# Seven products for the output gates of single-node LSTMs, with ScalarE's order held and GpSimd multiplying

## The chip, the cores and the metric

The kernel runs on one core of a Trainium2 chip. The core has TensorE (PE; its weight loads are listed as PEld), VectorE (DVE), ScalarE (ACT), GpSimd (POOL) and SyncE (SP, which issues DMA transfers here). Each takes its own instructions in order; between engines, semaphores make an instruction wait for what it reads or overwrites. The metric is the device time of one execution in microseconds (us), lower is better. Before the change the median of three runs is 2251.39 us (2249.25 to 2252.05).

## The reference

Four graph layers act on x (128 graphs of 64 nodes, 256 features). Each normalizes, applies ReLU, does its work and adds the result to x. The change lies in the third layer (layer 2, counted from 0). After two graph convolutions it runs four passes of LSTMs over windows of p = 1, 2, 3, 4 nodes and replaces the last node of each window by the LSTM's last state:

```python
def step(carry, x_t):
    h, c = carry
    g = x_t @ Wih.T + h @ Whh.T + bias
    i, f, gg, o = jnp.split(g, 4, axis=-1)
    c = jax.nn.sigmoid(f) * c + jax.nn.sigmoid(i) * jnp.tanh(gg)
    h = jax.nn.sigmoid(o) * jnp.tanh(c)
    return ((h, c), None)
...
for p in range(1, MAX_SKIP + 1):
    nw = Tv // p
    wins = h[:, :nw * p, :].reshape(Bv * nw, p, Hd)
    last = _lstm_last(Wih[p - 1], Whh[p - 1], bih[p - 1], bhh[p - 1], wins)
    idx = jnp.arange(nw) * p + (p - 1)
    h = h.at[:, idx, :].set(last.reshape(Bv, nw, Hd))
```

With p = 1 every node is a window, h and c begin at zero, and so there is one step without a forget gate: c = sigmoid(i) * tanh(gg), and the node becomes sigmoid(o) * tanh(c). Everything is float32.

## The kernel before

The kernel is one program without loops at run time. Instructions are written with tiles; a scheduler orders them on each engine by their place in the program and by what is ready in its own model of time, and puts in the semaphores. Three engines are wrapped (Ordered, line 789; Engines, line 811): mark gives the last instruction of TensorE, VectorE and ScalarE, and hold(marks) makes later instructions on an engine be issued behind the one given. GpSimd isn't wrapped. The wrapper's call, line 800, is the line under which nearly all instructions stand in the profile, so groups are told apart by tile names.

The features lie in four tiles big: 128 feature rows, two halves of the features (k), 64 nodes, 32 graphs; nodes(q) gives one. The sixteen blocks of x lie in tiles X0 to X15 of 1024 columns each (begin, line 1503). In layer 2 they are spilled to memory, and while the LSTMs run (windows, line 2268) their space serves as working store: weights, cells c (c_, a Ring, which hands out places in turn), states h, and differences.

A chunk is 16 nodes of one big tile, W = 256 columns for each half (h) of its graphs. In the pass p = 1 there are 16 chunks, taken in pairs; the loop over pairs calls lstm (line 2358) for each. A gate is a product of a 256 x 256 weight with 512 columns: as 2 x 2 blocks eight products of 128 x 128 with 256 columns. gates (line 2385) computes two gates at once with seven products instead. The weights' sums are made in weights (line 2296), the data's differences in the tile T (ls_tx). One set goes so:

- product 1 into bank a; ScalarE copies it to Z (ls_z)
- product 6 into bank b, VectorE adds it to Z; product 7 into bank f, VectorE makes U = Z + f in a part of X15; product 5 into bank d, and U + d is one quarter of the gate tile V (in ls_g)
- product 2 on top of bank a; ScalarE activates it into V: a second quarter
- product 4 on top of bank f, and Z + f is a third quarter; ScalarE activates the two quarters of the upper half k = 1
- product 3 on top of bank d, Z + d is the last quarter, and ScalarE's last activations finish it

Products 4 and 3 add to banks that VectorE has to have read by then; product 2 to one that ScalarE has read. There are seven banks.

Input gate and cell gate of a chunk are one such set. The output gate in p = 1 is computed apart, without savings, by eight of the plain products, as four matmuls of 512 columns (of both halves of the graphs), and activated from its banks. VectorE multiplies c; ScalarE takes tanh; last_state (line 2460) multiplies by the output gate on VectorE and writes the nodes in big, in runs of 16 columns.

The pass p = 2 uses other weight tiles; the weights of p = 3 are loaded into X4 to X7 and X0 to X3 after the first pair of p = 2.

Of the kernel before, what the change touches and what calls it, by code (L numbers as in the profile page):

```python
# [8 lines left out]
F32 = mybir.dt.float32  # L9
I32 = mybir.dt.int32  # L10
AF = mybir.ActivationFunctionType
ALU = mybir.AluOpType
# [901 lines left out]
class Fast:  # L914
# [28 lines left out]
    def act(self, out, a, f, **kw):  # L943
        return self.nc.scalar.activation(out, a, f, **kw)
# [499 lines left out]
B, N, D = 128, 64, 256  # L1444
P = 128
NB = 16
TPB = 4
BT = 512
# [18 lines left out]
class Kernel:  # L1467
# [35 lines left out]
    def begin(self):  # L1503
        nc, o, io = self.nc, self.o, self.io
        self.ident = self.c("ident", P, P)
        make_identity(nc, self.ident)
        self.ones = self.c("ones", P, P)
        nc.vector.memset(self.ones[:], 1.0)
        self.A, self.AT = self.c("A", N, N), self.c("AT", N, N)
        nc.sync.dma_start(self.A[:], io["adj"])  # L1510
        nc.sync.dma_start(self.AT[:], io["adj_t"])
        self.X = []
        for i in range(NB):
            self.X.append(self.c(f"X{i}", P, TPB, D))
        self.load_x(0)

    def load_x(self, i):
# [750 lines left out]
    def windows(self):  # L2268

        nc, o, io = self.nc, self.o, self.io
        cx, (w, wq, gp, tp, zp, psum, pst) = self.stage([("lsw", 1), ("lswq", 1), ("lsg", 2), ("lst", 2), ("lsz", 2),
                                                         ("lsps", 7), ("lstps", 1)], "tile")
        with cx:
            bias = w.tile([P, 4, 8], F32, name="ls_b")
            bh = w.tile([P, 4, 8], F32, name="ls_bh")
            with nc.allow_non_contiguous_dma("a few values"):
                nc.sync.dma_start(bias[:], io["L2_gnn_bih"].rearrange("q (k p) -> p q k", p=P))  # L2280
                nc.sync.dma_start(bh[:], io["L2_gnn_bhh"].rearrange("q (k p) -> p q k", p=P))
            o.add(bias[:], bias[:], bh[:])
            flat = [x[:].rearrange("p t d -> p (t d)") for x in self.X]
# [12 lines left out]
            def weights(p):  # L2296

                out = []
                for n, m in enumerate(("Wih", "Whh") if p > 1 else ("Wih",)):
                    t = load(None, n, None if p % 2 == 0 else 4 - 4 * n)  # L2300
                    ap = io[f"L2_gnn_{m}_t"][p - 1]
                    for kc in range(2):
                        nc.sync.dma_start(t[kc], ap[kc * P:(kc + 1) * P, :])
                    A = [[t[kc].rearrange("p (x k m) -> p x k m", k=2, m=P)[:, :, k, :] for kc in range(2)]
                         for k in range(2)]
                    S1, S2, S4 = (y.rearrange("p (x m) -> p x m", m=P) for y in t[2:5])
                    o.add(S1, A[1][0], A[1][1])
# [4 lines left out]
                    out.append({1: A[0][0], 2: A[0][1], 3: S4, 4: A[1][1], 5: S1, 6: S2, 7: S3,  # L2312
                                "A": A})
                return out

            ready = weights(1)
            for p in range(1, 5):
                Ws = ready
                nw = N // p
                parts = -(-nw // 16)  # L2320
                chunks = []
                for q in range(NG):
                    w0 = 0
                    for k in range(parts):
                        w1 = w0 + (nw - w0) // (parts - k)
# [32 lines left out]
    def lstm(self, p, t, ch, Ws):  # L2358


        o = self.o
        gp, tp, zp, psum, bias = self.lp
        w0, w1, H = ch["w0"], ch["w1"], self.nodes(ch["q"])
        nw = w1 - w0
        W = nw * 16
        at = slice(t + p * w0, t + p * (w1 - 1) + 1, p)
# [17 lines left out]

        def gates(xs, fs):
            G = gp.tile([P, 2, 1024], F32, name="ls_g")
            if p == 1 and len(xs) == 1:
                for k in range(2):
                    ps = psum.tile([P, BT], F32, name="ps")
                    for kc in range(2):  # L2390
                        self.mm(ps[:, 0:2 * W].rearrange("p (w b) -> p w b", b=32), Ws[0]["A"][k][kc][:, xs[0], :],
                                node(kc), kc == 0, kc == 1)
                    self.act(G[:, 0, 2 * W * k:2 * W * (k + 1)].rearrange("p (h w b) -> p h w b", h=2, b=16),
                             ps[:, 0:2 * W].rearrange("p (w h b) -> p h w b", h=2, b=16), fs[0],
                             bias=bias[:, p - 1, 2 * xs[0] + k:2 * xs[0] + k + 1])
# [61 lines left out]
        else:  # L2457
            self.last_state(H, at, W, s(G, 0), s(G, 1))

    def last_state(self, H, at, W, *factors):  # L2460
# [475 lines left out]
```

## Time and profile before

| | |
|---|---|
| median of three runs | 2251.39 us (2249.25 to 2252.05) |
| the profiled execution | 2249.32 us |
| its span | 2247.5 us |
| mean granted TensorE clock | 0.997 of full speed |
| TensorE, VectorE, ScalarE, GpSimd busy, us | 2207.4, 1629.2, 1153.4, 37.9 |
| pass p = 1 on TensorE | about 672 to 825 us |

The span runs from the first to the last instruction; the execution's time also holds what lies around it. Busy time of an engine is the sum of its instructions' time. Matmuls overlap, so the mean duration of one is longer than the distance from one to the next; each float32 matmul of the program is two instructions. Rows of the order of time give start, duration, engine, operation, out<-in, shape and count, and in brackets how long the engine had been idle and what released it. Rows of groups give the count, the busy time and the mean in ns, and the idle time ahead of them.

### The profile page before, as it was taken

Reading aid. Unit: us, or ns where it says so; the run is one execution under the profiler, and the core shown is the slowest. Engines: PE = TensorE matmul, PEld = TensorE weight load, DVE = VectorE, ACT = ScalarE, POOL = GpSimd, SP = SyncE. Lnnn points to the kernel's source line nnn. Section 1 sums busy time; section 2 is a strip of 40 time slices with the busy share of each in tenths; the row PEclk is TensorE's granted clock in tenths of the full one; section 3 lists DMA queues with packets and bytes.
Section 4 is the critical chain, followed back from the end, with each engine's and each line's share of the span. In section 5 each row is a group of like instructions: output and inputs, shape, how many; then the busy total and the mean of one; then the engine's idle time right before and its main releaser. Section 6 shows DMA issues by size and latency. Waiting matters only on the chain.

```text
span 2247.5 us, 33965 instructions
## 1 busy us (share of the span) xinstructions
PE 2207.4 (98%) x12683; PEld 1627.7 (72%) x12683; DVE 1629.2 (72%) x4132; ACT 1153.4 (51%) x2522; POOL 37.9 (2%) x66
## 2 busy tenths in 40 slices
PE   7999998999999999999999999999999999999999
PEld 4554445667987778888999999888888655555654
DVE  8877576888658776676766676656955787777767
ACT  5667865665545663444444444434634664444431
POOL 1000000000220000000000000000000000000000
PEclk9999999999999999999999999999999999999999
DMA  6000210121010000000100002000001000000001
GB/s 181 1 1 17 69 57 23 66 76 30 1 57 1 1 19 1 1 1 1 39 1 1 1 1 70 7 1 1 13 1 55 26 1 15 17 18 20 15 25 48
DMA packets 61071, 54.89 MB, mean 24 GB/s; under 512 B 15203, under 2 KB 58724, under 8 KB 60900
## 3 DMA queue, kind: packets, MB, share of 16 engines
q1 hardware_dynamic: 60900, 52.66, 7.5%
q8 instruction: 101, 1.65, 0.3%
q14 instruction: 70, 0.57, 0.1%
HBM read 35.86 MB, written 16.78 MB: 23 GB/s over the span
## 4 chain that ended last, share of the span: by engine, by line
PE 77%; DVE 5%; ACT 1%; issue 1%; DMA 0%; DVEq 0%; ACTq 0%; SPq 0%
PE ps L800 69%; PE pt L800 4%; PE acc L800 3%; PE pe L800 1%; DVE sm_m L800 1%; DVE X L800 1%; DVE aw L800 1%; DVE XV L800 0%; ACT ls_g L800 0%; ACT h L800 0%; DVE lin_s L800 0%; DVE ls_s L800 0%; DVE lin_p L800 0%; DMA ed_a<-in_L_gnn_a_dram 0%; DVE hT L800 0%
## 5 line engine op out<-in xcount | busy, mean ns | idle before, releaser
L800 ACT ACTIVATE ls_g<-ls_g,ls_b 128x512 f32<-128x512 f32 (+4 forms) x472 | 243.3, 565 | 147.7 <-DVE ls_g L800 145.7
L800 ACT ACTIVATE ls_g<-ps,ls_b 128x256 f32<-128x256 f32 (+3 forms) x268 | 115.4, 470 | 335.4 <-PE ps L800 331.9
L800 PE MATMUL ps<-z,w 128*128 128x512 f32 x512 | 255.5, 621 | 0.0
L800 PE MATMUL ps<-big,X 128*128 128x176 f32 (+3 forms) x848 | 212.9, 367 | 0.1
L800 DVE TENSOR_TENSOR ls_g<-ls_z,ps 128x512 f32<-128x512 f32 (+5 forms) x258 | 147.4, 577 | 90.3 <-PE ps L800 88.6
L800 PE MATMUL ps<-ls_tx,X 128*128 128x160 f32 (+2 forms) x960 | 207.0, 327 | 1.6 <-DVE ls_tx L800 0.9
L800 PE MATMUL ps<-X,X 128*128 128x160 f32 (+2 forms) x918 | 205.8, 308 | 0.0
L800 PE MATMUL ps<-X,ls_w 128*128 128x256 f32 x640 | 190.6, 379 | 0.1
L800 PEld LDWEIGHTS ps<-ls_tx,X 128*128 128x128 f32 x960 | 161.8, 190 | 16.4 <-DVE X L800 4.8
L800 DVE TENSOR_TENSOR aw<-at,ed_OST 128x1024 f32<-128x1024 f32 x128 | 150.3, 1220 | 28.7 <-PE ps L800 28.5
L800 PEld LDWEIGHTS ps<-big,X 128*128 128x128 f32 x848 | 146.1, 190 | 29.6 <-issue 19.1
L800 ACT ACTIVATE r<-ps 128x512 f32<-128x512 f32 x256 | 129.3, 625 | 74.4 <-PE ps L800 74.3
L800 DVE TENSOR_TENSOR X<-ls_g 128x1024 f32<-128x1024 f32 (+2 forms) x108 | 117.5, 1088 | 50.6 <-ACT ls_g L800 50.6
L800 PEld LDWEIGHTS ps<-X,X 128*128 128x128 f32 x918 | 152.8, 190 | 0.6
L800 PE MATMUL ps<-X,ls_s 128*128 128x256 f32 x480 | 142.8, 379 | 0.0
L800 PEld LDWEIGHTS ps<-z,w 128*128 128x128 f32 x512 | 87.0, 190 | 66.6 <-issue 59.5
L800 PE MATMUL ps<-ls_tx,ls_s 128*128 128x256 f32 x464 | 134.9, 380 | 0.0
L800 PEld LDWEIGHTS ps<-X,ls_w 128*128 128x128 f32 x640 | 121.5, 190 | 16.6 <-DVE X L800 0.5
L800 PE MATMUL ps<-ls_tx,ls_w 128*128 128x256 f32 x464 | 133.4, 380 | 0.0
L800 PE MATMUL ps<-big,ls_w 128*128 128x256 f32 x464 | 132.0, 380 | 0.7 <-ACT ls_z L800 0.7
L800 PE MATMUL ps<-ed_S,Q 64*128 64x512 f32 x512 | 121.0, 604 | 0.9 <-DVE X L800 0.9
L800 PE MATMUL ps<-aw,ed_ODT 128*32 128x512 f32 x1024 | 121.7, 593 | 0.1
(575 smaller groups left out, 4010.4 us busy)
## 6 DMA issues: line engine op xcount, KB each, us to landing
X<-in_x_dram SPq DMA_DIRECT2D x32, 512.0 KB
xs<-X SPq DMA_DIRECT2D x16, 512.0 KB
X<-xs SPq DMA_DIRECT2D x16, 512.0 KB
out_dram<-X SPq DMA_DIRECT2D x31, 256.0 KB
X<-in_L_gnn_Wih_t_dram SPq DMA_DIRECT2D x4, 512.0 KB
ls_w<-in_L_gnn_Wih_t_dram SPq DMA_DIRECT2D x4, 512.0 KB
ls_w<-in_L_gnn_Whh_t_dram SPq DMA_DIRECT2D x4, 512.0 KB
w<-in_L_gnn_W_t_dram SPq DMA_DIRECT2D x2, 512.0 KB
```

Source lines behind the costliest of these rows:

```text
L800: i = method(*a, **kw)
```

## The change

It concerns the pass p = 1 alone, which gets a function of its own, single, for a pair of chunks.

- A pair runs three sets of seven products: input and cell gate of the first chunk, those of the second, and the output gates of both chunks (the same weights, two data). The eight plain products go, and with them the weights' entry "A".
- The gate tiles come from a ring of four, each two X tiles (X8 and X9, X10 and X11, X12 and X13, X0 and X1). For that, X is allocated in eight tiles of two blocks, and X[i] is a half of one. T comes from a ring of three: X2, X3, X14.
- Instructions can be put off in the list late. The next set runs them right after its copy Z, and a hold puts ScalarE's part of them behind that copy: the last activations of a set, and the tanh of a cell, which follows one set after its product.
- GpSimd multiplies the cells, and the states in last_state. In the last pair the states are multiplied by VectorE, and the list is emptied at the end.
- In the output set two chunks share a bias, so one activation takes both.

```diff
-        self.X = []
-        for i in range(NB):
-            self.X.append(self.c(f"X{i}", P, TPB, D))
+        self.X2 = [self.c(f"X{i}", P, 2, TPB, D) for i in range(0, NB, 2)]
+        self.X = [x[:, i] for x in self.X2 for i in range(2)]
...
+            self.late = []
+            self.g_ = Ring([self.X2[i][:].rearrange("p x t d -> p x (t d)") for i in (4, 5, 6, 0)])
+            self.t_ = Ring([flat[i] for i in (2, 3, 14)])
...
+                    if p == 1:
+                        self.single(two, Ws[0], n + 2 >= len(chunks))
+                        continue
...
-            if p == 1 and len(xs) == 1:
-                for k in range(2):
-                    ps = psum.tile([P, BT], F32, name="ps")
-                    for kc in range(2):
-                        self.mm(ps[:, 0:2 * W].rearrange("p (w b) -> p w b", b=32), Ws[0]["A"][k][kc][:, xs[0], :],
-                                node(kc), kc == 0, kc == 1)
-                    self.act(G[:, 0, 2 * W * k:2 * W * (k + 1)].rearrange("p (h w b) -> p h w b", h=2, b=16),
-                             ps[:, 0:2 * W].rearrange("p (w h b) -> p h w b", h=2, b=16), fs[0],
-                             bias=bias[:, p - 1, 2 * xs[0] + k:2 * xs[0] + k + 1])
-                return G
...
+    def single(self, two, A, last):
+        nc, o = self.nc, self.o
+        _, _, zp, psum, bias = self.lp
+        I, F, G, O = range(4)
+        data = []
+        for ch in two:
+            H, at = self.nodes(ch["q"]), slice(ch["w0"], ch["w1"])
+            T = self.t_.next().rearrange("p (n w b) -> p n w b", n=4, b=16)
+            o.sub(T[:, 0:2], H[:, :, at, 16:32], H[:, 0, at, :].rearrange("p w (h b) -> p h w b", h=2))
+            o.sub(T[:, 2], H[:, 1, at, 16:32], T[:, 0])
+            o.sub(T[:, 3], H[:, 1, at, 0:16], T[:, 2])
+            data.append({1: H[:, 0, at, 0:16], 2: H[:, 1, at, 0:16], 3: H[:, 1, at, 16:32],
+                         5: T[:, 0], 7: T[:, 1], 6: T[:, 2], 4: T[:, 3]})
+
+        def gates(pairs, act):
...
+            a = product(1, "a", True)
+            self.act(Z, a, AF.Copy)
+            nc.hold((None, None, nc.mark()[2]))
+            while self.late:
+                self.late.pop(0)()
+            nc.hold()
+            o.add(Z, Z, product(6, "b", True))
+            o.add(U, Z, product(7, "f", True))
+            o.add(V[:, :, 1, 1], U, product(5, "d", True))
+            a = product(2, "a", False)
+            act(V[:, :, 0, 0], a, 0)
+            o.add(V[:, :, 1, 0], Z, product(4, "f", False))
+            act(V[:, :, 1], V[:, :, 1], 1)
+            o.add(V[:, :, 0, 1], Z, product(3, "d", False))
+            self.late.append(lambda: act(V[:, :, 0, 1], V[:, :, 0, 1], 0))
+            return tile
+
+        def apart(out, a, k):
+            for i, (x, f) in enumerate(((I, AF.Sigmoid), (G, AF.Tanh))):
+                self.act(out[:, i], a[:, i], f, bias=bias[:, 0, 2 * x + k:2 * x + k + 1])
+
+        def together(out, a, k):
+            self.act(out, a, AF.Sigmoid, bias=bias[:, 0, 2 * O + k:2 * O + k + 1])
+
+        def cell(V):
+            def product():
+                nc.gpsimd.tensor_tensor(V[:, 0], V[:, 0], V[:, 1], op=ALU.mult)
+                soon.append(lambda: self.act(V[:, 1], V[:, 0], AF.Tanh))
+            self.late.append(product)
+
+        cells, soon = [], []
+        for b in data:
+            V = gates(((I, b), (G, b)), apart)
+            self.late += soon
+            soon.clear()
+            cell(V)
+            cells.append(V)
+        V = gates([(O, b) for b in data], together)
+        self.late += soon
+        for i, ch in enumerate(two):
+            self.late.append(lambda i=i, ch=ch: self.last_state(
+                self.nodes(ch["q"]), slice(ch["w0"], ch["w1"]), 256, V[:, i], cells[i][:, 1],
+                engine=None if last else nc.gpsimd))
+        if last:
+            while self.late:
+                self.late.pop(0)()
+
+    def last_state(self, H, at, W, *factors, engine=None):
...
-            self.o.mul(y, *(x[:, 2 * W * k:2 * W * (k + 1)].rearrange("p (h w b) -> p h w b", h=2, b=16) for x in factors))
+            (engine or self.nc.vector).tensor_tensor(y, *(x[:, 2 * W * k:2 * W * (k + 1)].rearrange("p (h w b) -> p h w b", h=2, b=16) for x in factors), op=ALU.mult)
```

More of the change, by code (lines that the diff above doesn't have):

```diff
@@ L2282, in windows @@
             o.add(bias[:], bias[:], bh[:])
-            flat = [x[:].rearrange("p t d -> p (t d)") for x in self.X]
+            flat = [x.rearrange("p t d -> p (t d)") for x in self.X]
+            self.late = []
+            self.g_ = Ring([self.X2[i][:].rearrange("p x t d -> p x (t d)") for i in (4, 5, 6, 0)])
+            self.t_ = Ring([flat[i] for i in (2, 3, 14)])
             self.c_, self.h_, self.th_ = Ring(flat[12:15]), Ring(flat[8:10]), Ring(flat[10:12])
@@ L2311, in weights @@
                     o.sub(S3, A[0][0], A[1][0])
-                    out.append({1: A[0][0], 2: A[0][1], 3: S4, 4: A[1][1], 5: S1, 6: S2, 7: S3,
-                                "A": A})
+                    out.append({1: A[0][0], 2: A[0][1], 3: S4, 4: A[1][1], 5: S1, 6: S2, 7: S3})
                 return out
@@ L2458, in lstm, with product @@
             self.last_state(H, at, W, s(G, 0), s(G, 1))
-    def last_state(self, H, at, W, *factors):
+    def single(self, two, A, last):
[12 more added lines that the diff above has]
+        def gates(pairs, act):
+            tile = self.g_.next()
+            V = tile.rearrange("p x (k h w) -> p x k h w", k=2, h=2)
+            banks = {}
+            def product(m, bank, first):
+                if first:
+                    banks[bank] = psum.tile([P, 2, 256], F32, name="ps")
+                for i, (x, b) in enumerate(pairs):
+                    nc.tensor.matmul(banks[bank][:, i, :].rearrange("p (w b) -> p w b", b=16), A[m][:, x, :], b[m],
+                                     start=first and i == 0, stop=i == 1, skip_group_check=True)
+                return banks[bank][:]
+            Z = zp.tile([P, 2, 256], F32, name="ls_z")[:]
+            U = self.u_.next().rearrange("p (x w) -> p x w", x=2)
+            a = product(1, "a", True)
[40 more added lines that the diff above has]
+                self.late.pop(0)()
```

## The prediction

> **What bounds the kernel now.** I read the page first, for the engine that sets the time.
>
> ```profile
> PE 2207.4 (98%) x12683; PEld 1627.7 (72%) x12683; DVE 1629.2 (72%) x4132; ACT 1153.4 (51%) x2522; POOL 37.9 (2%) x66
> ...
> PE 77%; DVE 5%; ACT 1%; issue 1%; DMA 0%; DVEq 0%; ACTq 0%; SPq 0%
> ```
>
> TensorE is busy 98% of the span and carries 77% of the chain that ended last. But a busy TensorE says little of its rate, so next come stretches of the stage that changes (columns: stretch, length, then busy time and count of PE, PEld, DVE, ACT, POOL, the granted clock, DMA).
>
> ```profile
> 672.19:692.67 20.48, 19.49 (x75) 13.53 (x73) 18.88 (x33) 12.28 (x21) 0.00 (x0) 1.00 0.06 26
> 702.15:711.63 9.48, 9.48 (x38) 6.86 (x37) 7.09 (x11) 5.77 (x11) 0.00 (x0) 1.00 0.00 0
> 860.00:880.00 20.00, 20.00 (x94) 17.64 (x93) 10.71 (x16) 6.34 (x12) 0.00 (x0) 1.00 0.00 1
> ```
>
> The single-node stage starts at 672.2 with a pair of chunks that takes 20.48 us; after it every chunk takes 9.48 us, with TensorE always busy and the clock at 1.00. Each matmul of the program is two instructions here. A chunk issues 28 instructions of 256 columns (14 for input and cell gate, seven products each) and 8 of 512 columns (output gate, no saving). If a 512 costs two 256, that is 44 units in 9.48 us, 0.2155 us a unit; the two-node stage behind (94 instructions of 256 in 20 us) gives 0.2128. So the steady stage is limited by TensorE's issue rate, and a unit removed is worth 0.213 to 0.2155 us, so long as nobody makes TensorE wait.
>
> Who could is seen in the order of time of one chunk.
>
> ```profile
> 703.01 2.75 PE L800 MATMUL ps<-ls_tx,X 128*128 128x256 f32 x12
> 703.21 0.60 ACT L800 ACTIVATE ls_z<-ps 128x512 f32<-128x512 f32 x1 [0.18 <-PE ps L800]
> 704.14 0.69 DVE L800 TENSOR_TENSOR ls_z<-ls_z,ps 128x512 f32<-128x512 f32 x1 [0.55 <-PE ps L800]
> 704.78 1.29 DVE L800 TENSOR_TENSOR big<-ls_g 128x512 f32<-128x512 f32 x2
> 705.99 0.68 DVE L800 TENSOR_TENSOR X<-ls_z,ps 128x512 f32<-128x512 f32 x1
> 706.78 0.69 DVE L800 TENSOR_TENSOR ls_g<-X,ps 128x512 f32<-128x512 f32 x1
> 707.32 1.03 PE L800 MATMUL ps<-ls_tx,X 128*128 128x256 f32 x4
> 708.39 0.69 DVE L800 TENSOR_TENSOR ls_g<-ls_z,ps 128x512 f32<-128x512 f32 x1 [0.92 <-PE ps L800]
> 709.11 1.33 ACT L800 ACTIVATE ls_g<-ls_g,ls_b 128x512 f32<-128x512 f32 x2 [1.55 <-DVE ls_g L800]
> ```
>
> A set of seven products is a conversation: copy Z, three VectorE sums, and only then may products 4 and 3 go into banks that those sums read. The answer comes 0.2 to 0.27 us after the last matmul of a product. Now the output gate's eight instructions lie in these gaps. After the change nothing of that kind is left to fill them.
>
> **The change, part by part.** All per pair of chunks, eight pairs.
>
> *TensorE.* Output gates of two chunks: 16 instructions of 512 (32 units) become 28 of 256. 88 units become 84: 4 × 0.2155 = 0.86 us, or 0.85 by the lower rate. Over eight pairs -6.8 to -6.9 us; I take **-6.9**. The pair falls from 18.96 to 18.1 us, a set of seven to 6.03, a product to 0.86.
>
> *VectorE.* The rows for the prices (line group: shapes, count, busy, mean ns, idle before):
>
> ```profile
> L800 DVE TENSOR_TENSOR X<-ls_g 128x1024 f32<-128x1024 f32 x13 | 15.9, 1226 | 10.2 <-ACT ls_g L800 10.2
> L800 DVE TENSOR_TENSOR big<-ls_g 128x512 f32<-128x512 f32 x26 | 16.8, 689 | 0.1
> L800 ACT ACTIVATE ls_g<-X 128x1024 f32<-128x1024 f32 x13 | 13.6, 1048 | 0.0
> ...
> L2168 POOL TENSOR_TENSOR X<-a 128x512 f32<-128x512 f32 x11 | 13.9, 1267 | 264.6 <-ACT a L800 264.6
> ```
>
> Two cell products (1.226) and four state products (0.689) leave: -5.2. Three sets of five sums replace two sets: five more of 0.686, +3.4. From 14.2 busy (2 × 7.09) to 12.4 of 18.1: 69%. The final pair keeps its four state products on VectorE, 2.8 us, behind which only the next stage's sums queue.
>
> *ScalarE.* Four output activations of 0.676 leave (-2.7); a copy of 0.597, one activation of 512 from PSUM at 0.676, one of 1024 at 1.048 and one of 512 at 0.714 come (+3.0). 11.5 becomes 11.9 of 18.1: 66%. The hold places the previous set's last activations, and a tanh of 1.05, behind the new copy. What waits for them is a GpSimd product, a tanh one set later, or a state that a following set's tile reuse needs 2 us later. Nothing of TensorE's waits there. In front of the copy stay the activations of the upper half, 1.33 us for two, which start when the sum after product 4 ends: 0.06 into the next set. So copy at 1.4 to 2.0, sums at 2.05, 2.8 and 3.65, the last ending at 4.33. Product 4 is due at 4.30 and needs the second sum (3.5), product 3 at 5.16 needs the third: slack 0.8 us each. That cover hides all ScalarE edits; a copy 1 us later costs about 0.2 us a set.
>
> *GpSimd.* Two products of 1024 and four of 512. From 1.267 at 512 and 0.763 at 256 the first come to 2.3 us, an estimate. 2 × 2.3 + 4 × 1.27 = 9.7 of 18.1 us: 54%, in order: four state products, then one product in each of the next two sets. The first product has about 3 us until its tanh is queued, the rotating gate tiles (four) are written again about 2 us after the state product read them. Hidden, if GpSimd is alone.
>
> Against the move stands a rule: the Trainium skill, GPSIMD Engine Reference, § 4.1 Engine selection, gives elementwise products to VectorE, GpSimd being about 2 times slower. The row here says 1.84 (1267 over 689 ns), and left on VectorE they would make 17.6 busy of 18.1 us with a chain of waits in it, some 0.5 us of stall a set; so by the rule most of the gain would go, by the trace the move is needed.
>
> *GpSimd beside VectorE.* The trace shows one way in which they meet (order of time, layer 2):
>
> ```profile
> 557.74 1.27 POOL L2168 TENSOR_TENSOR X<-a 128x512 f32<-128x512 f32 x1 [193.76 <-ACT a L800]
> 559.08 2.32 POOL L2168 TENSOR_TENSOR X<-a,X 128x256 f32<-128x256 f32 x2
> 560.74 0.68 DVE L800 TENSOR_TENSOR n_r<-n_r,n_v 128x4 f32<-128x4 f32 x1
> ...
> 588.88 0.69 DVE L800 TENSOR_TENSOR y<-pt,w_b 128x512 f32<-128x512 f32 x1 [2.15 <-PE pt L800]
> ```
>
> The tiny n_r product, 0.16 us elsewhere, took 0.68 and ended at 561.42, as the GpSimd pair did (561.40): with both inputs in SBUF it sat until GpSimd was through. The y sum, one input from PSUM, took its usual 0.69 under a GpSimd instruction. So the sums of the products are free of this, and the six differences a pair of the T tiles (two of 0.685, four of 0.42, both inputs in SBUF) are not. VectorE is in order: a blocked difference holds the sums behind it, and those hold products 4 and 3. VectorE has two gaps of about 1.1 us a set; a difference leaves some 0.3 us of one, with 0.8 of slack that is 1.1 us of cover. A state product (1.27) is nearly always covered; a cell product can block up to 2.3, 1.2 beyond the cover. Ends: 0, and two such full blocks a pair, 2.4 us, 19 us in all. Cell products hold 26% of the time and some four groups of differences fall anywhere, so one hit a pair; its mean excess is 1.2² / (2 × 2.3) = 0.3. The differences become free only as the output set's products have read their tiles, 1 us or more into a cell product, so I take half, 0.15 a pair: **+1.2**.
>
> *Start.* The first pair of 20.48 loses 1.5 over the steady rate; 0.9 of it is TensorE waiting for ls_tx, whose space came free late. T now lies in X2, X3 and X14, free after the last layer-2 products at about 666. But eight weight sums (0.69, SBUF inputs) run in that pair and can meet GpSimd's first products. Between -1.5 and +1.5, **-0.4** taken, half of the wait.
>
> *X in pairs of tiles* adds no instruction; the halves don't overlap, so loads and spills of one need not wait for the other. SP's transfer of the third pass's second weight set into X0 to X3 now waits for the last states, some 4 us; used a whole pass later, its price is VectorE waiting in its sums, 0 to +1. I take 0.
>
> Sum: -6.9 + 1.2 - 0.4 = **-6.1 us**. The profiled execution took 2249.32 (span 2247.5 and 1.8 around it), which would become 2243.2; the median of the runs is 2.07 above it, so I predict 2251.39 - 6.1 = 2245.3.
>
> **The rivals.** *The lock eats the gain.* Groups of differences land in full cell products: 1.2 a pair, +9.6 instead of +1.2, so +2.3 in all; half as bad is -1.9. About 2251. For it: a cell product is as long as the two VectorE gaps together. Against: 31% idle VectorE.
>
> *Slower: GpSimd becomes a bound.* The state products write H in runs of 16 elements; the row of 1.267 has runs of 256. If that doubles them to 2.5, GpSimd is at 14.8 of 18.1 us and every difference meets it: each of four groups waits 0 to 2.5 us, a mean excess over the cover of 1.4² / (2 × 2.5) = 0.4, 1.6 a pair; with products late for their tanh about 2, so +16, and 2260. It decides from 0.86 + 0.05 + 0.56 = 1.5 us a pair on.
>
> *The hold doesn't bind.* With last activations still ahead of the copy it is 0.95 us later, 0.15 beyond the slack, 0.45 a pair, +3.6: 2249. With the tanh too (two sets in three) 1.2 in each, 2.5 a pair, +20: 2265. Against it: it is a plain order on one engine.
>
> **How the numbers follow.** Forecast 0.62, its own range 2242.8 to 2246.9; lock 0.21; GpSimd bound 0.10; hold 0.07. About 0.2% (4.5 us) is what a measurement can tell from no change. Faster by more: 0.62; slower: 0.10, 0.02 of the lock's and 0.02 of the hold's; within: 0.24. The range runs from -6.9 - 1.5 (2243, no stall and the start's whole loss back) to a little above the lock's 2251; what it leaves out is the GpSimd bound and the worse ends, 0.17.
>
> **What would show it.** Right: about 18.1 us from pair to pair, TensorE issuing 84 instructions in it, GpSimd about 54% busy, state products near 1.27. The lock: T differences far above 0.69 and 0.42 ending with GpSimd instructions, and TensorE waiting for VectorE's X or ls_g. The GpSimd bound: state products of 2 us and more. The hold: copies starting behind a tanh. Wrong altogether, if a time outside this stage moves by more than 2 us.

## The result: 0.23% slower, and the profile after

The changed kernel takes 2255.94 us (median of nine runs, 2252.99 to 2259.09), the kernel before, beside it, 2251.39. The ratio is 1.0023 with a 95% interval of 1.0015 to 1.0032: some 5 us slower, where 6 us faster were forecast. The profiled execution of after took 2253.03 us.

The page of after, its span, its engines and the chain that ended last, in which the time can't be seen yet:

```profile
span 2251.2 us, 34215 instructions
...
PE 2200.3 (98%) x12779; PEld 1641.8 (73%) x12779; DVE 1633.4 (73%) x4128; ACT 1155.1 (51%) x2522; POOL 112.5 (5%) x110
...
PE 74%; DVE 5%; issue 2%; ACT 1%; POOL 0%; DMA 0%; POOLq 0%; DVEq 0%; ACTq 0%; SPq 0%
```

TensorE is busy for 7.1 us less than before, as it should be with fewer columns to multiply, and the span is still 3.7 us longer. TensorE's share of the chain fell from 77% to 74%, which suggests that it now waits for somebody. Stretches of the stage, the first three pairs and one of the later ones (stretch, length, then busy time and count of PE, PEld, DVE, ACT, POOL, the granted clock, DMA):

```profile
669.94:689.97 20.03, 18.39 (x85) 15.87 (x84) 18.06 (x24) 11.06 (x19) 4.80 (x2) 1.00 0.01 1
689.97:712.47 22.50, 19.31 (x86) 15.53 (x84) 17.82 (x28) 11.94 (x21) 9.85 (x6) 1.00 0.00 0
712.47:733.90 21.43, 18.93 (x86) 15.70 (x85) 15.57 (x25) 11.73 (x21) 9.95 (x6) 1.00 0.00 1
792.00:811.37 19.37, 18.40 (x85) 15.88 (x84) 14.13 (x21) 11.80 (x21) 9.97 (x6) 1.00 0.00 1
```

84 instructions a pair are what was forecast (a window counts one more at its edge), but in place of the 18.1 us forecast the pair in the last row takes 19.37 us, and the second and third pair take 22.50 and 21.43. The clock is at 1.00 throughout, so the time goes into waits. Which, the waits of the stage tell (engine, tile and line; what it waited for; us in total, times, the longest):

```profile
POOL X L2513 <- DVE ls_z L800: 33.2, 12, 3.6
...
PEld ps L800 <- DVE X L800: 13.8, 10, 2.0
...
PE ps L800 <- DVE X L800: 9.8, 10, 1.6
DVE ls_tx L800 <- POOL big L2539: 4.0, 2, 2.6
...
PE ps L800 <- ACT ls_z L800: 1.5, 2, 1.1
```

TensorE waits ten times for VectorE's results in X (the gate tiles and U), and VectorE itself twice for nodes that GpSimd writes. The order of time shows both, and how regular they are. First an output set in the steady part (start, duration, engine, operation; in brackets the idle time ahead of it and what ended it):

```profile
805.97 2.36 POOL L2513 TENSOR_TENSOR X<-X 128x1024 f32<-128x1024 f32 x1 [3.63 <-DVE ls_z L800]
806.02 0.69 DVE L800 TENSOR_TENSOR X<-ls_z,ps 128x512 f32<-128x512 f32 x1
...
806.62 2.27 DVE L800 TENSOR_TENSOR X<-big 128x512 f32<-128x512 f32 x1
...
808.81 0.68 DVE L800 TENSOR_TENSOR X<-X,ps 128x512 f32<-128x512 f32 x1
...
809.54 1.99 PE L800 MATMUL ps<-big,X 128*128 128x256 f32 x8 [0.97 <-DVE X L800]
```

The second row is the sum U, the fourth the third sum, which has to read its bank before product 3 (the last row) may add to it. Between the two stands a difference for a T tile, X<-big. It takes 2.27 us instead of 0.69 and ends half a microsecond after GpSimd's cell product. Product 3 waits, and the set takes 7.29 us instead of 6.04: 1.25 us lost. The third sum would otherwise have stood at about 807.22 (806.02 + 1.20, the distance in a run below); it came 1.59 later and TensorE lost 1.25 of that, so the cover at this place was only 0.34 us.

The meeting is no accident. GpSimd's cell product reads what ScalarE's last activations of a set write; in 15 of 16 cases it starts 0.08 or 0.13 us after they end (0.48 at 742.24). The hold puts these activations behind the next set's copy Z, and that set's first sum (ls_z) waits for the copy too. In the steady pairs the two end within 0.02 us of each other, so the profile puts 12 of the 16 waits down to ls_z; that it isn't the releaser shows at 678.12, where the product starts 0.27 us before the first sum ends. So the product starts as the first sum ends, U follows that sum, and the difference follows U. The same happens in six output sets, 1.24 to 1.30 us each.

Second, the start of the stage and the first state products:

```profile
678.12 2.35 POOL L2513 TENSOR_TENSOR X<-X 128x1024 f32<-128x1024 f32 x1 [19.90 <-ACT X L800]
678.31 2.71 DVE L800 TENSOR_TENSOR ls_s<-ls_s,ls_w 128x512 f32<-128x512 f32 x1
...
681.67 1.13 PE L800 MATMUL ps<-X,X 128*128 128x256 f32 x4 [1.64 <-DVE X L800]
...
692.11 5.13 POOL L2539 TENSOR_TENSOR big<-X,X 128x512 f32<-128x512 f32 x4 [2.75 <-ACT X L800]
...
697.27 0.69 DVE L800 TENSOR_TENSOR ls_tx<-big 128x512 f32<-128x512 f32 x1 [1.43 <-POOL big L2539]
...
713.43 5.23 POOL L2539 TENSOR_TENSOR big<-X,X 128x512 f32<-128x512 f32 x4 [4.00 <-ACT X L800]
...
718.70 0.69 DVE L800 TENSOR_TENSOR ls_tx<-big 128x512 f32<-128x512 f32 x1 [2.61 <-POOL big L2539]
...
722.35 1.13 PE L800 MATMUL ps<-big,X 128*128 128x256 f32 x4 [1.08 <-ACT ls_z L800]
```

The first cell product blocks a weight sum (ls_s, 2.71 us for 0.69) and costs TensorE 1.9 us. The other rows are a wait that was not there before: the differences for the first chunks of the *next* pass (ls_tx) stand in VectorE's queue in the middle of p = 1. They read nodes that the state products write. Those products are now on GpSimd and end later, and VectorE, which takes its queue in order, stands idle 1.43 and 2.61 us with this pass's sums behind.

The groups of VectorE in the stage (count, busy time, mean ns, idle ahead), and then those of GpSimd, put sizes to it:

```profile
L800 DVE TENSOR_TENSOR X<-big 128x512 f32<-128x512 f32 x13 | 18.5, 1420 | 0.0
...
L800 DVE TENSOR_TENSOR X<-big,X 128x256 f32<-128x256 f32 x26 | 13.5, 520 | 0.3
```

```profile
L2513 POOL TENSOR_TENSOR X<-X 128x1024 f32<-128x1024 f32 x16 | 37.8, 2365 | 68.7 <-ACT X L800 35.5 <-DVE ls_z L800 33.2
L2539 POOL TENSOR_TENSOR big<-X,X 128x512 f32<-128x512 f32 x28 | 36.3, 1324 | 26.7 <-ACT X L800 26.7
```

**The account.** The length of the stage, from TensorE's first product of p = 1 to its first of p = 2, was 153.15 us and is 159.56: +6.4. A set without a stall takes 6.04 us; what the sets take above that is:

| what TensorE lost to | us |
|---|---|
| a difference of 512 columns behind a cell product, six output sets | 7.6 |
| a difference of 256 columns behind state products, second pair | 1.8 |
| ls_tx behind GpSimd's states, second and third pair | 3.3 |
| the weight sum behind the first cell product | 1.9 |
| sum | 14.6 |

Against it stand 6.9 us of saved matmuls and 1.5 us that the first pair had lost before: -6.9 - 1.5 + 14.6 = +6.2, of 6.4 measured. The last pair, which has no differences left to make, runs at 6.05 and 6.04 us a set.

The stage's length is the better measure in what follows, for the execution's time carries a scatter from ahead of the stage: the same instructions at the start of layer 2 began anywhere between 500.4 and 505.8 us in the twelve profiles (503.5 before, 500.6 after: 2.9 us that hide a part of the 6.4 in the two profiled executions).

### The profile page after: what moved, and what is told of

It reads as the page before. It is cut to its first block, busy times and chain, and to the rows that moved or that the text cites. A ratio compares the mean times of both kernels' runs of the same rounds, so it can differ in the third digit from the quotient of the medians.

```text
span 2251.2 us, 34215 instructions
## 1 busy us (share of the span) xinstructions
PE 2200.3 (98%) x12779; PEld 1641.8 (73%) x12779; DVE 1633.4 (73%) x4128; ACT 1155.1 (51%) x2522; POOL 112.5 (5%) x110
## 4 chain that ended last, share of the span: by engine, by line
PE 74%; DVE 5%; issue 2%; ACT 1%; POOL 0%; DMA 0%; POOLq 0%; DVEq 0%; ACTq 0%; SPq 0%
PE ps L800 67%; PE pt L800 4%; PE acc L800 3%; DVE X L800 2%; PE pe L800 1%; DVE sm_m L800 1%; DVE aw L800 1%; POOL big L2539 0%; ACT X L800 0%; DVE XV L800 0%; ACT ls_g L800 0%; ACT h L800 0%; ACT big L800 0%; DVE ls_z L800 0%; DVE lin_s L800 0%
## 5 line engine op out<-in xcount | busy, mean ns | idle before, releaser
L800 PE MATMUL ps<-X,X 128*128 128x160 f32 (+2 forms) x1302 | 296.7, 329 | 3.8 <-DVE X L800 3.8
L800 ACT ACTIVATE ls_g<-ls_g,ls_b 128x512 f32<-128x512 f32 (+5 forms) x408 | 207.9, 559 | 126.1 <-DVE ls_g L800 123.8
L800 PEld LDWEIGHTS ps<-X,X 128*128 128x128 f32 x1302 | 225.3, 190 | 15.7 <-DVE X L800 5.4
L800 ACT ACTIVATE ls_g<-ps,ls_b 128x256 f32<-128x256 f32 (+2 forms) x204 | 80.5, 438 | 303.7 <-PE ps L800 302.5
L800 PE MATMUL ps<-big,X 128*128 128x256 f32 (+2 forms) x816 | 182.1, 334 | 7.5 <-DVE X L800 5.9
L800 DVE TENSOR_TENSOR ls_g<-ls_z,ps 128x512 f32<-128x512 f32 (+3 forms) x226 | 125.5, 561 | 76.1 <-PE ps L800 74.3
L800 PEld LDWEIGHTS ps<-big,X 128*128 128x128 f32 x816 | 139.1, 190 | 18.8 <-DVE X L800 8.3
L800 PE MATMUL ps<-ls_tx,X 128*128 128x160 f32 (+1 forms) x704 | 146.2, 307 | 0.6 <-ACT ls_g L800 0.6
L800 DVE TENSOR_TENSOR X<-ls_z,ps 128x512 f32<-128x512 f32 (+4 forms) x185 | 112.7, 610 | 41.8 <-PE ps L800 37.9
L800 DVE TENSOR_TENSOR X<-ls_g 128x1024 f32<-128x1024 f32 (+2 forms) x92 | 97.9, 1064 | 38.9 <-ACT ls_g L800 38.9
```

Of the source, the lines that this page charges most:

```text
L800: i = method(*a, **kw)
```

## The experiments

Two mechanisms were suspected: the *lock* (a VectorE instruction with both inputs in SBUF sits until GpSimd is through) and the *queue* (ls_tx ahead of this pass's sums, waiting for GpSimd's states). The rivals were that the three sets of seven products are themselves too tight, that VectorE has too much work, and that ScalarE's hold costs more than it gives. All edits are to the changed kernel. Each ratio is to runs of the kernel before that were made beside the run, whose medians lie between 2248.74 and 2251.39 us, so times of different rows are compared by their ratios.

| kernel | stage, us | time, us | ratio to before (95%) |
|---|---|---|---|
| before | 153.15 | 2251.39 | 1 |
| after | 159.56 | 2255.94 | 1.0023 (1.0015 to 1.0032) |
| differences with an operand from PSUM | 149.56 | 2246.64 | 0.9980 (0.9971 to 0.9990) |
| ls_tx put off | 157.29 | 2254.30 | 1.0017 (1.0007 to 1.0027) |
| all products on VectorE | 144.87 (145.8) | 2240.64 | 0.9957 (0.9940 to 0.9974) |
| no hold | 169.61 | 2266.03 | 1.0066 (1.0049 to 1.0083) |
| cells on VectorE | 157.11 (158.1) | 2255.26 | 1.0025 (1.0015 to 1.0034) |
| states on VectorE | 156.85 | 2254.67 | 1.0023 (1.0012 to 1.0034) |
| differences on GpSimd | 158.10 | 2257.61 | 1.0039 (1.0025 to 1.0053) |
| all on VectorE, no hold | 145.00 (145.9) | 2239.56 | 0.9967 (0.9954 to 0.9980) |
| differences on GpSimd, ls_tx put off | 148.12 | 2245.25 | 0.9985 (0.9976 to 0.9995) |
| the seven products alone | 143.79 (145.6) | 2243.37 | 0.9967 (0.9956 to 0.9979) |

In four runs the schedule puts the first matmuls of p = 2 ahead of the last four of p = 1 (eight in the last run), so there the stage as measured ends early. The end of p = 1 in the last run shows it (matmuls with ls_w belong to p = 2):

```profile
817.62 0.59 PE L800 MATMUL ps<-big,ls_w 128*128 128x256 f32 x2
818.05 1.05 PE L800 MATMUL ps<-X,X 128*128 128x256 f32 x4
818.94 0.59 PE L800 MATMUL ps<-big,ls_w 128*128 128x256 f32 x2
819.38 1.09 PE L800 MATMUL ps<-big,X 128*128 128x256 f32 x4
```

In brackets is the time to the last matmul of p = 1, less that of the matmuls of p = 2 before it. Comparisons go by these.

### The lock: differences with one operand from PSUM

```diff
-            o.sub(T[:, 0:2], H[:, :, at, 16:32], H[:, 0, at, :].rearrange("p w (h b) -> p h w b", h=2))
-            o.sub(T[:, 2], H[:, 1, at, 16:32], T[:, 0])
-            o.sub(T[:, 3], H[:, 1, at, 0:16], T[:, 2])
+            o.sub(T[:, 0:2], H[:, :, at, 16:32], self.flat0[:, 0:512].rearrange("p (k w b) -> p k w b", k=2, b=16))
+            o.sub(T[:, 2], T[:, 0], self.flat0[:, 0:256].rearrange("p (w b) -> p w b", b=16))
+            o.sub(T[:, 3], T[:, 2], self.flat0[:, 256:512].rearrange("p (w b) -> p w b", b=16))
```

(flat0 is a bank of zeros in PSUM; the tiles T then hold no differences, and the output is not the reference's.)

> The six differences a pair take their second operand from a PSUM bank of zeros, so that they have one input in SBUF (the products then get wrong data, and the output is not the reference's); their number, shapes and engine stay. Measured by the stage's length, from TensorE's first product of p = 1 to its first of p = 2 (before 153.1 us, after 159.6). Lock theory (a difference with two SBUF inputs sits until GpSimd's instruction ends, and holds the sums behind it): the differences return to 0.69 and 0.42 us, the stall of 1.25 us in each output set (six of them, 7.6 us) and the one of 1.8 in the second pair go, the stage is 150 +- 1.5, the time 9 us under the changed kernel and 4 under the one before. Rival (VectorE's order alone: a difference stands between the second and the third sum and delays product 3 whatever GpSimd does): differences are already 0.7 us, the stage stays within 2 us of 159.6.

The stage took 149.56 us, 10.0 less than after, where the account gives 7.6 + 1.8 = 9.4 to the lock. The groups of VectorE in this run, and then the same place in the order of time:

```profile
L800 DVE TENSOR_TENSOR X<-X,pt 128x256 f32<-128x256 f32 x31 | 13.0, 418 | 1.1
L800 DVE TENSOR_TENSOR X<-big,pt 128x512 f32<-128x512 f32 x15 | 10.2, 680 | 0.0
```

```profile
710.41 0.69 DVE L800 TENSOR_TENSOR X<-ls_z,ps 128x512 f32<-128x512 f32 x1
710.42 2.38 POOL L2515 TENSOR_TENSOR X<-X 128x1024 f32<-128x1024 f32 x1 [2.92 <-DVE ls_z L800]
...
711.01 0.68 DVE L800 TENSOR_TENSOR X<-big,pt 128x512 f32<-128x512 f32 x1
...
711.61 0.68 DVE L800 TENSOR_TENSOR X<-X,ps 128x512 f32<-128x512 f32 x1
```

The difference stands between the same two sums, with a cell product running on GpSimd, and takes 0.68 us: 1420 became 680 ns, 520 became 418, and the output set takes 6.04. So neither the order on VectorE nor the count of its instructions makes the stall, but the second operand in SBUF. This is what the Trainium skill says (SBUF — State Buffer, § Who interferes with whom): a VectorE instruction with two SBUF inputs contends with a GpSimd instruction that reads SBUF; one with a single SBUF input, outside the 2-port modes, does not.

### The queue: ls_tx put off

```diff
+        if p == 2 and t == 0:
+            self.nc.hold((None, self.guard, None))
         o.sub(T[:, 0:2], H[:, :, at, 16:32], half(0))
...
+        self.nc.hold()
...
+        self.guard = nc.mark()[1]
         V = gates([(O, b) for b in data], together)
```

> Only the differences of the next pass's first two chunks (ls_tx) are issued later on VectorE, behind the sums that precede the last output set of p = 1; in the changed kernel they stand in the second and third pair, where VectorE waits for GpSimd's states that they read. Queue theory (VectorE in order waits there 1.4 and 2.6 us and lets products 2 and 4 come late): the sets that are 1.3 and 2.0 us too long become 6.04, the stage is 156.3 +- 0.7, the time 3 us under the changed kernel. Rival (those two stalls come from the lock on the differences around them): the stage stays at 159.6 within 0.7.

157.29 us: 2.3 gained of the 3.3. Up to the end of p = 1 only the ls_tx rows moved in VectorE's order. Both sets, 7.33 and 8.05 us in after, take 6.04, as the queue theory has it. What is missing is a new stall of 1.2 us in the last set, where one of the moved rows meets a cell product (1.98 us for 0.42). The pair of runs with GpSimd's differences below tests the same edit on a longer wait.

### Nothing on GpSimd

```diff
             def product():
-                nc.gpsimd.tensor_tensor(V[:, 0], V[:, 0], V[:, 1], op=ALU.mult)
+                o.mul(V[:, 0], V[:, 0], V[:, 1])
...
-                engine=None if last else nc.gpsimd))
+                engine=None))
```

> Cells and states are multiplied by VectorE, nothing by GpSimd; all else as changed. Lock theory: no difference is longer than 0.75 us and no wait for GpSimd is left, but VectorE has 17.6 us of work for 18.1; with waits in its chain about 0.3 us are lost a set, 19 us a pair, the stage is 153 +- 3, so 4 to 9 us under the changed kernel, near the one before. Rival (the move to GpSimd is worth more than the lock costs, as the prediction had it): the stage is 162 or more, slower than the changed kernel.

144.87 us (145.8 with the last matmuls), 7 better than expected, and 2240.64: of the runs so far that compute everything, the first that beats both kernels, by 0.4% over the one before. A long stretch of the stage in this run, and then the same stretch of before:

```profile
690.00:800.00 110.00, 110.00 (x510) 95.86 (x509) 103.84 (x171) 70.97 (x120) 0.00 (x0) 1.00 0.00 1
```

```profile
690.00:800.00 110.00, 110.00 (x420) 79.58 (x419) 82.54 (x129) 68.40 (x118) 0.00 (x0) 1.00 0.00 1
```

TensorE never waits in 110 us and issues 510 instructions, of 256 columns each. VectorE's rows cover 94% of the stretch, yet TensorE doesn't wait for it. (The busy time of a stretch counts a moment once, however many rows cover it; it is not the sum of the rows, as was said ahead of the prediction. Their sum here is 115.3 us.) Two groups of this run, and four state products in its order of time:

```profile
L800 DVE TENSOR_TENSOR X<-X 128x1024 f32<-128x1024 f32 x16 | 19.5, 1221 | 0.4 <-ACT X L800 0.3
...
L800 DVE TENSOR_TENSOR X<-big 128x512 f32<-128x512 f32 x13 | 8.9, 687 | 0.1
```

```profile
692.48 2.50 DVE L800 TENSOR_TENSOR big<-X,X 128x512 f32<-128x512 f32 x4
```

The differences are back at 687 ns, and a cell product costs VectorE 1.22 us where GpSimd takes 2.36. Four products of 0.688 each took 2.50 us together: they start 0.60 apart, so the rows overlap, and both their sum and the time that they cover overstate how full VectorE is.

### The hold

```diff
             self.act(Z, a, AF.Copy)
-            nc.hold((None, None, nc.mark()[2]))
             while self.late:
                 self.late.pop(0)()
-            nc.hold()
```

> The hold on ScalarE is left out: last activations, the tanh and the rest of the list may be issued ahead of the next set's copy. If the hold binds and matters, copies start 0.9 us later or more in most sets and the stage grows by 0.45 a pair, 3.6 us, to 163. If the scheduler puts the copy first anyway, or the 0.8 us of slack covers it: within 1 us of 159.6. The lock theory expects the stall of 1.25 in the output sets unchanged in both.

169.61 us, 10.0 more than after, where 3.6 were expected. The order of time, two tanh rows on ScalarE:

```profile
773.94 1.06 ACT L800 ACTIVATE X<-X 128x1024 f32<-128x1024 f32 x1 [2.52 <-POOL X L2511]
...
780.69 1.06 ACT L800 ACTIVATE X<-X 128x1024 f32<-128x1024 f32 x1 [2.47 <-POOL X L2511]
```

Without the hold ScalarE takes a tanh while its product is still on GpSimd, and stands for 2.5 us with the activations of the current set and the next copy behind it. In the four steady pairs whose output sets stall this costs 3.4 us more than in after. The other 6.7 lie in the first three pairs, and not all of them are ScalarE's: VectorE's order changed as well (ls_tx stands ahead of a third sum and waits 5.6 us instead of 4.0; a difference of the first pair now meets a cell product), and twice the granted clock was at half for 3.4 us, which the run with GpSimd's differences explains below. How the 6.7 divide was not tried. With GpSimd multiplying, the hold is needed. Whether it is worth anything by itself, the same edit without GpSimd tells:

```diff
-            nc.hold((None, None, nc.mark()[2]))
...
-            nc.hold()
...
-                nc.gpsimd.tensor_tensor(V[:, 0], V[:, 0], V[:, 1], op=ALU.mult)
+                o.mul(V[:, 0], V[:, 0], V[:, 1])
...
-                engine=None if last else nc.gpsimd))
+                engine=None))
```

> Nothing on GpSimd and no hold on ScalarE. With GpSimd the hold was worth 10 us of stage, since without it a tanh that waited 2.5 us for GpSimd's product stood ahead of ScalarE's other work. If that wait was the cause, the hold is worth little here: stage 145 to 147, as with the hold (144.9). If the copy's place alone is what counts, as the prediction reckoned it: 148 to 155.

145.00 against 144.87 us (145.9 against 145.8): nothing. The hold pays for a delay that the move to GpSimd made.

### One half of GpSimd's work each

Cells on VectorE, states on GpSimd:

```diff
-                nc.gpsimd.tensor_tensor(V[:, 0], V[:, 0], V[:, 1], op=ALU.mult)
+                o.mul(V[:, 0], V[:, 0], V[:, 1])
```

> Cells are multiplied by VectorE, states still by GpSimd. Lock theory: what blocked the difference of 512 in each output set for 2.3 us was the cell product, so those stalls (1.25 each) go; a state product blocks at most 1.27, mostly covered; the next pass's differences still wait for GpSimd's states (2 to 3 us in all). Stage 149 +- 2 (changed kernel 159.6, nothing on GpSimd 144.9), time about 10 us under the changed kernel. Rival (VectorE fuller by 2.4 us a pair is late for the chain): stage 155 or more.

157.11 us (158.1 with the last matmuls), and 149 was expected: a miss. The groups of VectorE, and the order of time of one pair:

```profile
L800 DVE TENSOR_TENSOR X<-big,X 128x256 f32<-128x256 f32 x26 | 21.6, 830 | 0.0
...
L800 DVE TENSOR_TENSOR X<-big 128x512 f32<-128x512 f32 x13 | 9.0, 710 | 0.1
```

```profile
793.75 5.53 POOL L2539 TENSOR_TENSOR big<-X,X 128x512 f32<-128x512 f32 x4 [14.25 <-ACT X L800]
...
794.21 1.10 DVE L800 TENSOR_TENSOR X<-big,X 128x256 f32<-128x256 f32 x1
...
795.83 0.91 DVE L800 TENSOR_TENSOR X<-big,X 128x256 f32<-128x256 f32 x1
```

The 512 differences are free, as they no longer meet cell products. But the 256 ones now stand in VectorE's order behind the first state products and meet all four, one after the other: 0.83 us on average instead of 0.42. By this trace the lock moved to other instructions with the schedule. The wait of ls_tx stayed too, at 4.2 us. The states on VectorE, cells on GpSimd:

```diff
-                engine=None if last else nc.gpsimd))
+                engine=None))
```

> States are multiplied by VectorE, cells still by GpSimd. Lock theory: the cell product goes on blocking the difference in the output set, about 1.25 us a pair, and the weight sum in the first pair, 1.9; the waits of the next pass's differences for GpSimd go. Stage 145 + 7.6 + 1.9 = 154.5 +- 2, time about 5 us under the changed kernel. Rival (the states' four blocks a pair are the greater part): stage 148 or less.

156.85 us, where 154.5 with a margin of 2 was expected: 0.35 beyond it. VectorE's group in this run:

```profile
L800 DVE TENSOR_TENSOR X<-big 128x512 f32<-128x512 f32 x13 | 18.7, 1440 | 0.0
```

The cell products block the 512 differences as in after (1440 ns), some 1.3 us in each output set. There is no wait for ls_tx, since VectorE writes the nodes itself. Neither half alone brings the kernel under the time before.

### GpSimd makes the differences as well

If the lock is between GpSimd and VectorE's differences, giving GpSimd the differences too removes it, at the price of more work on GpSimd and later states.

```diff
-            o.sub(T[:, 0:2], H[:, :, at, 16:32], H[:, 0, at, :].rearrange("p w (h b) -> p h w b", h=2))
...
+            sub = lambda out, a, b: nc.gpsimd.tensor_tensor(out, a, b, op=ALU.subtract)
+            sub(T[:, 0:2], H[:, :, at, 16:32], H[:, 0, at, :].rearrange("p w (h b) -> p h w b", h=2))
...
```

> The six differences a pair go to GpSimd as well, where no lock can meet them; products stay on GpSimd, which then has 15.3 us of work for 18.1 in one queue, while VectorE keeps only sums with a PSUM input (and the eight weight sums). Lock theory: no VectorE instruction in the steady pairs is longer than 0.75 us, and the stall of 1.25 in each output set goes; what is left is GpSimd being late with a difference or a product. Stage 147 to 153. Rival (GpSimd's own queue is what is slow): stage above 158, TensorE or ScalarE waiting for GpSimd.

158.10 us, above what was expected and just the rival's number. But GpSimd's queue is slow in the first pairs alone. In a steady stretch of this run TensorE has no wait:

```profile
730.00:790.00 60.00, 60.00 (x278) 52.77 (x277) 34.38 (x50) 38.86 (x66) 46.28 (x37) 0.99 0.00 1
```

Sets take 6.04 and 6.05 us there, 77% of GpSimd's time being busy. All is lost in the first three pairs: 1.9 us at the weight sum, and two sets of 11.75 and 11.49 us, whose wait on VectorE is

```profile
DVE ls_tx L800 <- POOL big L2540: 10.3, 2, 5.4
```

GpSimd makes differences ahead of its state products, so ls_tx waits 10.3 us for them instead of 4.0. TensorE in turn stands still for 3.7 and 3.2 us, and what follows each time is part of the price (the first of the two; then two stretches of the same length behind it):

```profile
703.14 1.93 PE L800 MATMUL ps<-big,X 128*128 128x256 f32 x4 [3.74 <-ACT ls_z L800]
```

```profile
703.33:706.74 3.41, 3.41 (x9) 2.50 (x9) 1.85 (x3) 1.40 (x4) 2.36 (x1) 0.50 0.00 0
706.74:710.15 3.41, 3.41 (x18) 3.00 (x17) 2.00 (x3) 2.59 (x6) 0.00 (x0) 1.00 0.00 0
```

The granted clock was at half for 3.41 us, in which TensorE issued 9 instructions; in the next 3.41 us it issued 18. That is some 1.7 us lost behind each wait, an estimate from these counts, so of the 11.2 us that the two sets are too long about a third is the clock's.

The last question is then whether that wait is all. The same with the edit that puts ls_tx off:

> Differences on GpSimd, as in the run before it, and the next pass's differences issued late. With the differences on GpSimd the steady pairs already took 18.13 us, the rate of TensorE, and nearly all of the loss (two sets of 11.7 and 11.5 us) came while VectorE waited 10.3 us for GpSimd's states ahead of those differences. Queue theory: both sets become 6.04, the stage 158.1 - 11.2 = 147, the first pair's weight sum (1.9) being what is left; the time is 6 us under the kernel before. Rival (GpSimd, with 85% of its time taken, is late elsewhere once this wait is gone): stage above 151.

148.12 us, 1 from what was expected, and 2245.25: 0.15% faster than before, with GpSimd multiplying and subtracting for 84% of the steady time (50.14 of 60 us in the same stretch). What is left above the steady rate is the weight sum's 1.9 us and 1.2 in the last set, where a moved ls_tx row meets a cell product. The clock stays at full speed. So the 10 us between the two runs all came of ls_tx's wait, the half clock behind it included, and in the steady sets a busy GpSimd cost nothing once VectorE had no difference to make beside it and waited for nothing that GpSimd writes.

### The seven products alone

```diff
             self.act(Z, a, AF.Copy)
-            nc.hold((None, None, nc.mark()[2]))
-            while self.late:
-                self.late.pop(0)()
-            nc.hold()
...
-            self.late.append(lambda: act(V[:, :, 0, 1], V[:, :, 0, 1], 0))
+            act(V[:, :, 0, 1], V[:, :, 0, 1], 0)
...
+            o.mul(V[:, 0], V[:, 0], V[:, 1])
+            self.act(V[:, 1], V[:, 0], AF.Tanh)
...
+            self.last_state(self.nodes(ch["q"]), slice(ch["w0"], ch["w1"]), 256, V[:, i], cells[i][:, 1])
```

No list, no hold, nothing on GpSimd: each instruction where it comes in the program.

> Only the three sets of seven products and the new tiles are kept: nothing on GpSimd, no hold, no list of late instructions; each cell product, tanh and state is written in the program right behind what it needs. Theory (VectorE has room for all products, and what the list and the hold buy is needed only with GpSimd): stage 145 to 147, time 8 us under the kernel before. Rival (it takes the late list to keep the copy early): 150 or more, a gain of 3 us or less.

143.79 us as measured, 145.6 to the last matmul of p = 1: 7.6 under before and as short as the other two versions without GpSimd. The time is 2243.37 us, a ratio of 0.9967 (0.9956 to 0.9979). In their times the three can't be told apart, as their intervals overlap. The products of the output gates bring the whole gain; of the other two parts of the change one costs it and the other is there to limit that cost.

## Why the prediction was wrong

- **TensorE, -6.9: right.** 84 instructions a pair, a set of 6.04 where nothing waits (forecast 6.03). With nothing on GpSimd the stage is 7.3 to 7.6 us shorter than before: the 6.9, the 1.5 of the start, and 0.5 to 0.9 lost in small gaps.
- **GpSimd beside VectorE, +1.2: this step failed.** The mechanism was named, and the size was wrong: 9.4 us measured, 7.6 by cell products and 1.8 by state products, which were taken as nearly always covered. The step treated the differences as falling anywhere, with a mean excess of 0.3 a hit, and then halved it. But the place is fixed by the program: GpSimd starts as the set's first sum ends, the difference comes one sum later, 0.65 us into the cell product, in six pairs of eight. And the cover of 1.1 us was that of a gap plus slack; between U and the third sum there is no gap, the difference itself takes 0.6 of the slack, and 0.34 was left. One full block a pair is the rival that the lock eats the gain: it gave 1.2 us a pair and 9.6 in all; 1.25 and 9.4 were measured. That the totals agree so well is in part luck, as the block comes in six pairs, and the second pair's 1.8 makes up for the others.
- **A wait that was not in the sum at all: +3.3.** The change moves the state products to a slower engine behind other work, and instructions of the next pass that read the states stand in VectorE's queue in the middle of this one. The prediction looked for what is queued behind the moved work on its own engine and not for who reads its result.
- **Start, -0.4: +0.4 measured.** All of the old 1.5 came back, but the weight sum that the step named met the first cell product and cost 1.9.
- **"Left on VectorE ... some 0.5 us of stall a set": wrong.** In the run without GpSimd TensorE's gaps make some 0.8 us in the whole stage. VectorE's rows cover 17.1 us a pair there (94% of 18.13), near the 17.6; but as the rows overlap, that left room. The rule that the prediction weighed and set aside (the Trainium skill, GPSIMD Engine Reference, § 4.1 Engine selection: elementwise products belong on VectorE, GpSimd being about 2 times slower) gave the right choice here: with all products on VectorE the gain stays (145.8 us of stage), with them on GpSimd as in the change it goes (159.56). The ratio of 2 agrees (2.36 over 1.22 us for a cell product, 1.9), but by the account it was not the slowness itself that cost the gain; it was the lock and the queue.
- **GpSimd's sizes: right.** 2.3 us forecast for the cell product and 2.36 measured, 1.27 for the state product and 1.32. The rival with state products of 2.5 us is refuted. (Its 14.8 us of work adds up to 14.6 by its own rows.)
- **The hold: it binds, as forecast,** but its worth was misread. Without it 10.0 us are lost, where the prediction had 3.6 and 20 for its two cases. In the steady pairs ScalarE then waits for GpSimd and doesn't merely come late by its own work; and without GpSimd the hold is worth nothing.
- **X in pairs and SP's transfer, 0: nothing found there.** The waits of the stage show one on a DMA, of 0.3 us. The criterion that a time outside the stage should not move by 2 us was of no use: executions differ by up to 5 us ahead of the stage with the same instructions.

The sum by these terms: forecast -6.9 + 1.2 - 0.4 = -6.1; measured -6.9 + 9.4 + 3.3 + 0.4 = +6.2.

## What to carry to other kernels

Before moving an elementwise product to GpSimd, look in the order of time at what VectorE does just behind the instruction that releases it: in this kernel an instruction with both inputs in SBUF that stood there paid for what was left of GpSimd's instruction, every time, and what counted as cover was the slack at that very place. Then look for all readers of the moved result, later stages included, that an in-order engine may have queued ahead of urgent work. And try the core of a change without its companions: here they were what made it slower.

## What the runs showed of the hardware that was not expected

- Consecutive VectorE instructions of 512 float32 columns, 0.688 us in their own rows, start 0.60 apart (four in 2.50 us). With its rows covering 94% of 110 us, VectorE did not hold up TensorE.
- A blocked difference ends after GpSimd's instruction by most of its own time: 2.27 us from 806.62, GpSimd through at 808.33, the difference at 808.89, 0.56 later. A blocked difference of 256 columns, 0.42 us when free, ended 0.28 later (687.66 to 689.64, GpSimd through at 689.36). It seems to do its work only once the lock is free; that was not tested by itself.
- The granted clock fell to half for 3.4 us after each of four gaps of 2.8 to 4.1 us, from start to start, between TensorE's matmuls (two without the hold, two with GpSimd's differences). In the stages of the other ten profiles no gap is over 2.1 us, and the clock stays at 1.00. A long stall so cost more than its own length.
- An execution's time differs by some 5 us, ahead of the changed code, between profiles of kernels that have the same instructions there. A part of it is the clock: from 100 to 200 us its mean is 0.97 or 0.98 in five of the twelve profiles (0.98 before) and 1.00 in the others (1.00 after), and the matmuls there come 1.6 to 3.3 us later. What sets the clock there, and the rest, stays open.
